# Norm order, fillers and a buffer pool in a four-layer gated cross-attention kernel

## The chip, the cores and the metric

The kernel runs on one core of one Trainium2 chip. The metric is device time in microseconds (us) of one execution; lower is better. The core's engines are TensorE (PE in the profile, with its weight loads as PEld), VectorE (DVE), ScalarE (ACT), GpSimd (POOL) and SyncE (SP, which issues most DMAs).

## What is computed

Two batches of 256 tokens of 256 features (x) pass four layers, each a cross-attention to a context of 2 x 512 rows and a feed-forward, both added to x through a gate. In front of each stands a layer norm.

```python
x = x + tanh(g_xattn[0]) * L0_xattn(layernorm(x), ctx)   # 16 heads, no weights
x = x + tanh(g_ffn[0])   * L0_ffn(layernorm(x), ...)     # ternary weights, SiLU gate
x = x + tanh(g_xattn[1]) * L1_xattn(layernorm(x), ctx, Wq, Wk, Wv, Wo)  # 16 heads of 128
x = x + tanh(g_ffn[1])   * L1_ffn(layernorm(x), ...)     # dense, SiLU gate
x = x + tanh(g_xattn[2]) * L2_xattn(layernorm(x), ctx, ...)  # linear attention
x = x + tanh(g_ffn[2])   * L2_ffn(layernorm(x), ...)     # 8 experts, one for each token
x = x + tanh(g_xattn[3]) * L3_xattn(layernorm(x), ctx, mask)
x = x + tanh(g_ffn[3])   * L3_ffn(layernorm(x), ...)     # shared expert + 2 of 8 experts
```

## The kernel before

The 512 tokens are four tiles of 128 (`n`), two for each batch. All layers are written out one after the other in one function, `flamingo`; each is a chain of products on TensorE into PSUM, evictions and activations on ScalarE, and sums on VectorE. PSUM has two `acc` buffers, four `mm` buffers and two `tr` buffers (for transposes). In SBUF, pools `q4` (11 buffers), `q2` (15) and `q1` (4) are shared by all stages; a tile waits until a buffer of its pool is released.

A scheduler orders the instructions of each engine and places the waits. Where its order is not wanted, the text ties them: `behind(i, j)` puts i after j on the same engine without a wait, and `inline` does so for one instruction after the other. There are three such lines: `line` for VectorE, `pool_line` for GpSimd and `pe_line` for TensorE. An empty list means that the order is free; `append(None)` starts a new line, `clear()` ends it.

The places that the change touches:

- **First feed-forward** (`ternary_ffn`, L660 to L743). Eight chunks `c`. Each has its SiLU, a product with the gate, and `halves` (L370): VectorE cuts the result to its upper bits (`top`), ScalarE copies that as the high half, and GpSimd subtracts for the low half. `l0_down(c)` (L693) multiplies both halves.
- **End of the second attention** (L935 to L1053). The last two heads, 14 and 15, are added to x by tiles: `add14`, `add15` for tiles 0 and 1; `late14`, `late15` for 2 and 3. `norm_stats` (two instructions on VectorE, two on GpSimd for the root) and `norm_apply` (L234) prepare the second feed-forward, `turned1` transposes a tile into `xT`. In between stand constant tables for the routing to come (an iota on GpSimd, L982, its conversion on VectorE, L983, and what is made of it), and the first keys and values of the third attention (`early_products`, `early_keys2`). `pause1` is called inside the feed-forward after its first chunks.
- **Routing** of layer 2 (L1265 to L1340). `busy(cols)` multiplies `ident` by columns of the iota into a part of a PSUM tile that nobody reads. It stands between the norms of tiles 2 and 3, their transposes and their logits. `places` (L1235) then counts rows by experts, `there2` makes a selection matrix, `gather_first` (L1263) gathers rows into `xsT`.
- **Experts of layer 2** (L1421 to L1501). Six quads of four blocks of 32 rows: `l2_up`, `l2_turn`, `l2_down`, `l2_mask`, and `l2_back` (L1471), which multiplies a quad's rows back to the tokens. It sums in two PSUM tiles `y`, tokens' tiles 0 and 1 in one, 2 and 3 in the other.
- **Fourth attention** (L1505 to L1595). `l3_stats(n)` adds y to x and takes the norm's statistics, `norm_apply`, `l3_turned` (L1537), `l3_scores`, `l3_exps` (L1551). The small sum `none` (L1517 to L1521) tells which batch has no valid row. `load_table` runs one activation on a single column so that the table of a function is loaded then.
- **Experts of layer 3** (`l3_down`, L1776). Ten blocks; each is copied from PSUM to a tile `o3` and scattered to DRAM by GpSimd (`scatter`, L1666). All four reads of the scattered rows (L1834) wait for every scatter; the final sums and the stores follow.

Of the kernel before, what the change touches and what calls it, by code (L numbers as in the profile page):

```python
# [25 lines left out]
P = 128  # L26
# [24 lines left out]
def flamingo(ctx: ExitStack, tc: tile.TileContext, a: dict, out: bass.AP):  # L51
# [181 lines left out]
    def norm_apply(n, xn, stats):  # L233
        return inline(nc.vector.tensor_scalar(xn[:, n, :], x[:, n, :], *stats, ALU.subtract, ALU.mult))  # L234
# [37 lines left out]
    def mm(shape=None):  # L272
        return ps_mm.tile(shape or [P, 512], F32, tag="mm", name="mm")
# [95 lines left out]

    def halves(hi, lo, v):  # L370

        top = q2.tile([P, T], F32, tag="q2", name="top")
        i = nc.vector.tensor_scalar(top.bitcast(I32), v.bitcast(I32), -4096, None, ALU.bitwise_and)
        j = nc.scalar.copy(hi, top)
        nc.gpsimd.tensor_sub(lo, v, top)
        return i, j
# [283 lines left out]
    def ternary_ffn():  # L660
# [36 lines left out]
        for c, _, ts in by_batch(FCH):  # L697
# [15 lines left out]
            if ts.stop == T:  # L713
                s = q2.tile([P, T], F32, tag="q2", name="silu")
                silu = nc.scalar.activation(s, ps[c][0], AF.Silu, scale=scales[0])
                nc.vector.tensor_mul(s, s, ps[c][1])
                h = q4.tile([P, 2, T], F32R, tag="q4", name="hT")
                if c > 1:
                    behind(silu, copied, "its product waits for that copy")
                last, copied = halves(h[:, 0, :], h[:, 1, :], s)  # L720
                if c == 1:
                    line.append(last)
                    ternary_signs(1)
                    line.clear()
# [232 lines left out]
    sums = small.tile([P, 2, 1], F32, tag="sum1", name="sum1", bufs=2)  # L957
    nc.scalar.copy(sums, den)
    late14(scale, 2)
    norm_apply(0, xn, stats1[0])  # L960
    late14(scale, 3)
    norm_apply(1, xn, stats1[1])
    scale = l1_scales(sums, 2)
    for n in (2, 3):
        late15(scale, n, 0)
        stats1[n] = norm_stats(n)
    ctx_nat = nat.tile([P, B, 2, 2 * D], F32, tag="nat", name="ctx_nat3")
    ctxT = turned_ctx.tile([P, B, 2, M], F32, tag="ctxT", name="ctxT2")
# [6 lines left out]
    for b in range(B):  # L975
        load_context(nc.sync, ctx_nat, b)


    SL = QUADS * P
    iota = q4.tile([P, SL + 1], F32, tag="q4", name="iota")  # L980
    iota_i = q4.tile([P, SL + 1], I32, tag="q4", name="iota_i")
    nc.gpsimd.iota(iota_i, pattern=[[1, SL + 1]], base=0, channel_multiplier=0)  # L982
    nc.vector.tensor_copy(iota, iota_i)  # L983
    own = small.tile([P, QUADS], F32, tag="own", name="own", bufs=1)
    own_i = small.tile([P, QUADS], I32, tag="own_i", name="own_i", bufs=1)
    nc.gpsimd.iota(own_i, pattern=[[P, QUADS]], base=1, channel_multiplier=1)
    nc.gpsimd.tensor_copy(own, own_i)
    upto = small.tile([P, E, E], F32, tag="upto", name="upto", bufs=1)
    nc.vector.tensor_tensor(upto, iota[:, 0:E].unsqueeze(1).to_broadcast([P, E, E]),
                            iota[:, 0:E].unsqueeze(2).to_broadcast([P, E, E]), ALU.is_le)  # L990

    near1 = small.tile([P, E], F32, tag="near", name="near", bufs=1)
    far = small.tile([P, E], F32, tag="far", name="far", bufs=1)
    nc.vector.tensor_copy(near1, iota[:, 1:512:64])
    nc.vector.tensor_scalar(far, near1, -1.0, 449.0, ALU.mult, ALU.add)
    over = small.tile([P, E], F32, tag="over", name="over", bufs=1)
    nc.vector.tensor_scalar_add(over, near1, 64.0)

    near_r = small.tile([P, NT, E], F32R, tag="near_r", name="near_r", bufs=1)
    nc.vector.tensor_scalar_mul(near_r, near1.unsqueeze(1).to_broadcast([P, NT, E]), 1.0 / P)  # L1000
    fit2 = const.tile([P, 1], F32, name="fit2")
    ids = small.tile([P, 2 * NT], I32, tag="ids", name="ids", bufs=1)
    nc.gpsimd.iota(ids, pattern=[[2 * P, NT], [1, 2]], base=0, channel_multiplier=2)

# [33 lines left out]
    def pause1(ci, b):  # L1038
        if (ci, b) == (1, 0):
            early_keys2(1, *early_products(1))  # L1040
            for n in (2, 3):
                turned1(n)
        if (ci, b) == (1, 1):
            for t in (line, pool_line, pe_line):
                t.clear()

    kv0 = early_products(0)
    for n in (2, 3):
        norm_apply(n, xn, stats1[n])
    for n in range(2):  # L1050
# [251 lines left out]

    busy(384)
    turned = []
    for n in (2, 3):
        norm_apply(n, xn, stats2[n - 2])
        turned.append(logits2(n))
        if n == 2:
            busy(256)
    for fn in turned:  # L1310
        fn()
    busy(384)
    load_dn2(2)
# [107 lines left out]
    def l2_up(q):  # L1421
# [10 lines left out]
        s = q2.tile([P, T], F32, tag="q2", name="silu")  # L1432
        nc.scalar.activation(s, pa, AF.Silu)
        h = q2.tile([P, T], F32, tag="q2", name="h2")
# [8 lines left out]
    def l2_down(q, hT):  # L1443
# [15 lines left out]
        return o  # L1459

    def l2_mask(q):
        back = q2.tile([P, T], F32R, tag="q2", name="back")
        nc.vector.tensor_scalar(back, row, own[:, q : q + 1], None, ALU.is_equal)
        return back

    def l2_back(q, o, back, y):
        for n in range(NT):
            for i in range(2):


                inline(nc.tensor.matmul(y[n // 2][:, n % 2, :], lhsT=back[:, n * P : (n + 1) * P], rhs=o[:, i, :],  # L1471
                                        start=(q == 0 and n % 2 == 0 and i == 0),
                                        stop=(q == QUADS - 1 and n % 2 == 1 and i == 1)), pe_line)

# [4 lines left out]
    for q in range(QUADS + 2):  # L1479
# [18 lines left out]
        if q < QUADS:  # L1498
            hTs[q] = l2_turn(h)
        if q >= 2:  # L1500
            l2_back(q - 2, os.pop(q - 2), backs.pop(q - 2), y)  # L1501
    pe_line.clear()
    late = pair(1, "late").rearrange("p s c -> p (s c)")
# [13 lines left out]
    none = const.tile([P, B], F32, name="none")  # L1517
    p = ps_tr.tile([P, B, 4], F32, tag="tr", name="tr")
    nc.tensor.matmul(p.rearrange("p b c -> p (b c)"), lhsT=ones, rhs=named, start=True, stop=True)
    nc.vector.reduce_sum(none, p, axis=AX.X)  # L1520
    nc.vector.tensor_scalar(none, none, 0.0, None, ALU.is_le)  # L1521

    for t in (line, pe_line):
        t.append(None)
    xn = q4.tile([P, NT, D], F32, tag="q4", name="xn")
# [58 lines left out]
    norm_apply(2, xn, stats3[2])  # L1584
    norm_apply(3, xn, stats3[3])
    l3_turned(0)
    l3_scores(0, ps3[0], slice(0, P), [0])
# [188 lines left out]
    def l3_down(q, hT):  # L1776
        acc = ps_acc.tile([P, D], F32, tag="acc", name="acc")
        for c in range(2):
            for j in range(4):
# [734 lines left out]
```

## Time and profile before

| | us |
|---|---|
| median of 3 runs | 574.4 |
| lowest, highest | 572.72, 577.37 |
| profiled execution | 578.8 |
| its span | 577.1 |
| TensorE busy in the span | 552.9 |
| VectorE, ScalarE, GpSimd busy | 323.9, 227.1, 131.5 |
| mean granted TensorE clock | 0.984 |

The profile is one execution; its span runs from the first instruction to the last. A row of the timeline has the start (us from the span's start), the time in us, engine, line, operation, what it writes and reads with shapes, how many instructions are merged, and in brackets the engine's idle time before it with what ended it. A matrix product in fp32 of 256 columns appears as two instructions. "PEclk" is the granted TensorE clock, in tenths of the full speed on the page and as a fraction in tables by stretches.

### The profile page before, as it was taken

The numbers are of one execution on the slowest core, as the hardware profiler recorded it, in microseconds if no ns is written. First come the engines' busy times: TensorE is split into PE (matmuls) and PEld (weight loads), VectorE is DVE, ScalarE is ACT, GpSimd is POOL, SyncE is SP. The second block draws the span as 40 slices with busy tenths as digits, with TensorE's granted clock in tenths as the row PEclk, the third lists the DMA queues.
The fourth block names the chain that finished last, engine by engine and source line by source line (L and its number), as shares of the span: only waits on it lengthen the run. The fifth ranks groups of instructions, "written<-read, shape, count | busy, mean of one in ns | idle before, by whom it ended". The sixth has DMA issues, their size and how long they took to land.

```text
span 577.1 us, 8662 instructions
## 1 busy us (share of the span) xinstructions
PE 552.9 (96%) x3302; PEld 399.9 (69%) x3302; DVE 323.9 (56%) x744; ACT 227.1 (39%) x465; POOL 131.5 (23%) x227
## 2 busy tenths in 40 slices
PE   8999999999999999999999999999989998999994
PEld 6555665888878788888878776476676456884453
DVE  6968798645475554845555665234566336462323
ACT  6876445643444445344444424113322211522310
POOL 3885444111031101211011123011130002151240
PEclk9999999999999999999999999999997998899998
DMA  7900300000004000130033229630031999313013
GB/s 303 408 5 0 125 22 1 1 1 0 1 0 146 0 2 1 19 128 1 0 147 147 73 72 351 252 147 0 6 141 61 378 420 379 91 45 114 18 44 124
DMA packets 16073, 60.20 MB, mean 104 GB/s; under 512 B 2686, under 2 KB 5957, under 8 KB 12391
## 3 DMA queue, kind: packets, MB, share of 16 engines
q1 hardware_dynamic: 13974, 54.75, 25.3%
q0 software_dynamic: 1472, 4.28, 2.0%
q10 hardware_dynamic: 576, 0.53, 0.3%
q8 instruction: 28, 0.46, 0.3%
q14 instruction: 23, 0.18, 0.1%
HBM read 54.75 MB, written 5.25 MB: 104 GB/s over the span
## 4 chain that ended last, share of the span: by engine, by line
PE 84%; DVE 7%; ACT 2%; issue 2%; POOL 2%; DMA 2%; POOLq 0%; ACTq 0%; DVEq 0%; SPq 0%
PE mm L277 26%; PE acc L277 18%; PE mm L607 8%; PE mm L609 4%; PE mm L1426 4%; PE s L452 3%; PE acc L464 2%; PE q L607 2%; PE mm L1760 2%; PE acc L1447 2%; DVE x L280 2%; PE q L609 1%; PE mm L1263 1%; PE y L1471 1%; PE acc L1782 1%
## 5 line engine op out<-in xcount | busy, mean ns | idle before, releaser
L277 PE MATMUL mm<-qT,kT 128*128 128x256 f32 x256 | 60.7, 380 | 0.0
L277 PE MATMUL acc<-e,v 128*128 128x256 f32 x256 | 60.5, 379 | 0.0
L600 POOL TENSOR_TENSOR h_parts<-w,h_top 128x256 fp32r<-128x256 f32 x28 | 21.8, 779 | 161.6 <-PE acc L277 86.7
L277 PEld LDWEIGHTS mm<-qT,kT 128*128 128x128 f32 x256 | 48.1, 190 | 9.2 <-ACT oT L792 1.6
L277 PEld LDWEIGHTS acc<-e,v 128*128 128x128 f32 x256 | 48.3, 189 | 7.9 <-ACT e L781 0.2
L781 ACT ACTIVATE e<-mm 128x512 f32<-128x512 f32 x64 | 38.0, 597 | 25.8 <-PE mm L277 25.7
L784 DVE TENSOR_TENSOR t<-e,e 128x512 f32<-128x512 f32 x32 | 22.1, 691 | 28.4 <-ACT e L781 28.4
L456 ACT ACTIVATE e<-s 128x512 f32<-128x512 f32 x64 | 32.8, 607 | 6.7 <-PE s L452 5.5
L229 POOL TENSOR_TENSOR rstd<-mv,eps_ln 128x1 f32<-128x1 f32 x30 | 8.1, 270 | 98.6 <-DVE mv L228 98.6
L277 PE MATMUL mm<-xT,ffn 128*128 128x512 f32 (+1 forms) x80 | 28.0, 510 | 1.3 <-ACT xT L1036 1.3
L277 PE MATMUL acc<-w,oT 128*128 128x256 f32 x112 | 27.2, 386 | 2.1 <-ACT oT L792 2.1
L612 ACT ACTIVATE v<-mm 128x512 f32<-128x512 f32 x24 | 14.3, 597 | 33.7 <-PE mm L609 33.7
L613 DVE SCALAR_TENSOR_TENSOR v<-mm,v 128x512 f32<-128x512 f32 x24 | 16.6, 692 | 19.0 <-ACT v L612 19.0
L607 PE MATMUL mm<-ctx_top,h_parts 128*128 128x512 f32 x56 | 27.3, 487 | 0.0
L280 DVE SCALAR_TENSOR_TENSOR x<-acc,gsum,x 128x256 f32<-128x256 f32 x56 | 24.1, 479 | 4.8 <-PE acc L277 4.8
L792 ACT COPY oT<-acc 128x256 f32<-128x256 f32 x32 | 11.9, 372 | 33.4 <-PE acc L277 33.4
L277 PEld LDWEIGHTS acc<-w,oT 128*128 128x128 f32 x112 | 20.7, 190 | 6.3 <-ACT oT L792 3.7
L612 ACT ACTIVATE kT<-mm 128x512 f32<-128x512 f32 x28 | 16.7, 598 | 20.6 <-PE mm L609 20.6
L277 PEld LDWEIGHTS mm<-xT,ffn 128*128 128x128 f32 x80 | 15.0, 190 | 13.6 <-issue 11.0
L452 PE MATMUL s<-w_q,ctx_nat 32*128 32x256 f32 x256 | 21.8, 403 | 2.0 <-ACT e L456 1.1
L613 DVE SCALAR_TENSOR_TENSOR kT<-mm,kT 128x512 f32<-128x512 f32 x28 | 19.3, 689 | 7.2 <-ACT kT L612 7.2
L1426 PE MATMUL mm<-gu,xsT 128*32 128x512 f32 x192 | 22.4, 595 | 0.2 <-ACT xsT L1381 0.2
(393 smaller groups left out, 1162.5 us busy)
## 6 DMA issues: line engine op xcount, KB each, us to landing
gu<-in_l_gu_all SPq DMA_DIRECT2D x16, 1024.0 KB, 7.0
w<-in_l_all SPq DMA_DIRECT2D x4, 2048.0 KB, 13.0
dn<-in_l_dn_all SPq DMA_DIRECT2D x4, 1024.0 KB, 6.2
dn<-in_l_dn_all SPq DMA_DIRECT2D x8, 512.0 KB, 9.7
gu<-in_l_gu SPq DMA_DIRECT2D x4, 704.0 KB, 11.1
ctx_nat<-in_ctx SPq DMA_DIRECT2D x4, 512.0 KB, 13.2
ctxT<-in_ctxT SPq DMA_DIRECT2D x4, 512.0 KB, 5.4
sh<-in_l_sh SPq DMA_DIRECT2D x2, 704.0 KB, 8.5
```

The lines of the kernel that those rows point to most:

```text
L277: inline(nc.tensor.matmul(dst, lhsT=lhsT, rhs=rhs, start=(i == 0), stop=(i == len(pairs) - 1)), pe_line)
L280: return inline(nc.vector.scalar_tensor_tensor(x[:, n, cols], acc, scalar, x[:, n, cols], ALU.mult, ALU.add))
L452: in_turn(nc.tensor.matmul(ps[j][:, k, :], lhsT=ctx_nat[rows, b, hf, c * P : (c + 1) * P], rhs=qm[rows, n, i, :], start=True, stop=True))
L456: exps.append(nc.scalar.activation(es[j], ps[j], AF.Exp))
L600: nc.gpsimd.tensor_sub(dst[1], src, t)
L607: inline(nc.tensor.matmul(same, lhsT=left(i, k), rhs=right(i, k), start=(k == 0 and i == 0), stop=(k == 1 and i == 1)), pe_line)
L609: inline(nc.tensor.matmul(cross, lhsT=left(2, k), rhs=right(2, k), start=(k == 0), stop=(k == 1)), pe_line)
L612: nc.scalar.mul(dst, cross, -EPS * scale)
L613: return inline(nc.vector.scalar_tensor_tensor(dst, same, (1.0 + EPS) * scale, dst, ALU.mult, ALU.add))
L781: nc.scalar.activation(e, s, AF.Exp)
L784: nc.vector.tensor_add(t, es[0], es[1])
L1426: inline(nc.tensor.matmul(ps[j * BLK : (j + 1) * BLK, :], lhsT=xsT[k][:, (4 * q + j) * BLK : (4 * q + j + 1) * BLK], rhs=gu2[home(q, j)][: ...
```

## The change

- `halves` gets the engine of its subtraction as an argument; chunk 0 of the first feed-forward uses VectorE, the others GpSimd as before.
- At the end of the second attention `norm_apply(0)` stands ahead of `late14(2)`, and `norm_apply(1)` ahead of `late14(3)`. The block with `k2`, `v2`, `early_products(0)` and the norms of tiles 2 and 3 moves in the text ahead of the tables; the iota is put behind the last root on GpSimd, its conversion behind the last norm on VectorE.
- In `pause1` the transposes of tiles 2 and 3 stand ahead of the second pair of key and value products.
- In the routing, `busy(384)` becomes twice `busy(256)`; `busy(256)` between the norms becomes `busy(384)`; and `busy(256)` follows each of the two logits, instead of one `busy(384)` after both.
- The last rows of layer 2's experts go back by tiles: quad 4 for tiles 0 and 1, then quad 5 for 0 and 1, then both for 2 and 3. The table of exponentials is loaded after the last SiLU. Three products `ones` x `woT2`, which nobody reads, follow the last of them on TensorE. The sum `none` moves behind the four norms and into the lines.
- `o3` comes from `q2` instead of `q1`.

```diff
-    def halves(hi, lo, v):
+    def halves(hi, lo, v, engine):
...
-        nc.gpsimd.tensor_sub(lo, v, top)
+        engine.tensor_sub(lo, v, top)
...
-                last, copied = halves(h[:, 0, :], h[:, 1, :], s)
+                last, copied = halves(h[:, 0, :], h[:, 1, :], s, nc.gpsimd if c else nc.vector)
...
     nc.scalar.copy(sums, den)
+    norm_apply(0, xn, stats1[0])
     late14(scale, 2)
-    norm_apply(0, xn, stats1[0])
+    norm_apply(1, xn, stats1[1])
     late14(scale, 3)
-    norm_apply(1, xn, stats1[1])
...
+    roots1 = pool_line[-1]
...
     def pause1(ci, b):
         if (ci, b) == (1, 0):
-            early_keys2(1, *early_products(1))
             for n in (2, 3):
                 turned1(n)
+            early_keys2(1, *early_products(1))
...
+    kv0 = early_products(0)
+    for n in (2, 3):
+        normed[:] = [norm_apply(n, xn, stats1[n])]
...
-    nc.gpsimd.iota(iota_i, pattern=[[1, SL + 1]], base=0, channel_multiplier=0)
-    nc.vector.tensor_copy(iota, iota_i)
+    behind(nc.gpsimd.iota(iota_i, pattern=[[1, SL + 1]], base=0, channel_multiplier=0), roots1, "not among the norms")
+    behind(nc.vector.tensor_copy(iota, iota_i), normed[0], "not among the norms")
...
-    busy(384)
+    for _ in range(2):
+        busy(256)
     turned = []
     for n in (2, 3):
         norm_apply(n, xn, stats2[n - 2])
         turned.append(logits2(n))
         if n == 2:
-            busy(256)
+            busy(384)
     for fn in turned:
         fn()
-    busy(384)
+        busy(256)
...
-        nc.scalar.activation(s, pa, AF.Silu)
+        silus[:] = [nc.scalar.activation(s, pa, AF.Silu)]
...
-    def l2_back(q, o, back, y):
-        for n in range(NT):
+    def l2_back(q, o, back, y, tiles=range(NT)):
+        for n in tiles:
...
-        if q >= 2:
+        if 2 <= q < QUADS:
             l2_back(q - 2, os.pop(q - 2), backs.pop(q - 2), y)
+        if q == QUADS:
+            l2_back(4, os[4], backs[4], y, (0, 1))
+            load_table(AF.Exp, silus[0], "the table of exponentials")
+    for tiles in ((0, 1), (2, 3)):
+        if tiles[0]:
+            l2_back(4, os[4], backs[4], y, tiles)
+        l2_back(5, os[5], backs[5], y, tiles)
...
-    for t in (line, pe_line):
-        t.append(None)
+    line.append(None)
+    pe_line.append(last_back[0])
+    warm = mm([P, D])
+    for _ in range(3):
+        chain(warm, [(ones, woT2[:, 0, :])])
...
     norm_apply(3, xn, stats3[3])
+    p = ps_tr.tile([P, B, 4], F32, tag="tr", name="tr")
+    chain(p.rearrange("p b c -> p (b c)"), [(ones, named)])
+    inline(nc.vector.reduce_sum(none, p, axis=AX.X))
+    inline(nc.vector.tensor_scalar(none, none, 0.0, None, ALU.is_le))
...
-        o = q1.tile([P, D], F32, tag="q1", name="o3")
+        o = q2.tile([P, D], F32, tag="q2", name="o3")
```

More of the change, by code (lines that the diff above doesn't have):

```diff
@@ L976, in flamingo @@
         load_context(nc.sync, ctx_nat, b)
[L979 to L982, printed above, removed]
-    nc.vector.tensor_copy(iota, iota_i)
[L984 to L1003, printed above, removed]
     k2 = [q4.tile([P, 4, D], F32, tag="q4", name="k2")]
@@ L1048, in flamingo @@
     for n in (2, 3):
-        norm_apply(n, xn, stats1[n])
+        normed[:] = [norm_apply(n, xn, stats1[n])]
+    SL = QUADS * P
+    iota = q4.tile([P, SL + 1], F32, tag="q4", name="iota")
+    iota_i = q4.tile([P, SL + 1], I32, tag="q4", name="iota_i")
+    behind(nc.gpsimd.iota(iota_i, pattern=[[1, SL + 1]], base=0, channel_multiplier=0), roots1, "not among the norms")
+    behind(nc.vector.tensor_copy(iota, iota_i), normed[0], "not among the norms")
+    own = small.tile([P, QUADS], F32, tag="own", name="own", bufs=1)
+    own_i = small.tile([P, QUADS], I32, tag="own_i", name="own_i", bufs=1)
+    nc.gpsimd.iota(own_i, pattern=[[P, QUADS]], base=1, channel_multiplier=1)
+    nc.gpsimd.tensor_copy(own, own_i)
+    upto = small.tile([P, E, E], F32, tag="upto", name="upto", bufs=1)
+    nc.vector.tensor_tensor(upto, iota[:, 0:E].unsqueeze(1).to_broadcast([P, E, E]),
+                            iota[:, 0:E].unsqueeze(2).to_broadcast([P, E, E]), ALU.is_le)
+    near1 = small.tile([P, E], F32, tag="near", name="near", bufs=1)
+    far = small.tile([P, E], F32, tag="far", name="far", bufs=1)
+    nc.vector.tensor_copy(near1, iota[:, 1:512:64])
+    nc.vector.tensor_scalar(far, near1, -1.0, 449.0, ALU.mult, ALU.add)
+    over = small.tile([P, E], F32, tag="over", name="over", bufs=1)
+    nc.vector.tensor_scalar_add(over, near1, 64.0)
+    near_r = small.tile([P, NT, E], F32R, tag="near_r", name="near_r", bufs=1)
+    nc.vector.tensor_scalar_mul(near_r, near1.unsqueeze(1).to_broadcast([P, NT, E]), 1.0 / P)
+    fit2 = const.tile([P, 1], F32, name="fit2")
+    ids = small.tile([P, 2 * NT], I32, tag="ids", name="ids", bufs=1)
+    nc.gpsimd.iota(ids, pattern=[[2 * P, NT], [1, 2]], base=0, channel_multiplier=2)
     for n in range(2):
@@ L1459, in l2_down @@
         return o
+    last_back = []
     def l2_mask(q):
@@ L1464, in l2_mask @@
         return back
-    def l2_back(q, o, back, y):
-        for n in range(NT):
+    def l2_back(q, o, back, y, tiles=range(NT)):
+        for n in tiles:
             for i in range(2):
-                inline(nc.tensor.matmul(y[n // 2][:, n % 2, :], lhsT=back[:, n * P : (n + 1) * P], rhs=o[:, i, :],
+                last_back[:] = [inline(nc.tensor.matmul(y[n // 2][:, n % 2, :], lhsT=back[:, n * P : (n + 1) * P], rhs=o[:, i, :],
                                         start=(q == 0 and n % 2 == 0 and i == 0),
-                                        stop=(q == QUADS - 1 and n % 2 == 1 and i == 1)), pe_line)
+                                        stop=(q == QUADS - 1 and n % 2 == 1 and i == 1)), pe_line)]
     y = [ps_acc.tile([P, 2, D], F32, tag="acc", name="y2") for _ in range(2)]
@@ L1517, in flamingo @@
     none = const.tile([P, B], F32, name="none")
[L1518 to L1521, printed above, removed]
-    for t in (line, pe_line):
-        t.append(None)
+    line.append(None)
[3 more added lines that the diff above has]
+        chain(warm, [(ones, woT2[:, 0, :])])
     xn = q4.tile([P, NT, D], F32, tag="q4", name="xn")
```

## The prediction

> **What bounds the kernel now.** I read the page first: engine shares, then the clock row.
>
> ```profile
> PE 552.9 (96%) x3302; PEld 399.9 (69%) x3302; DVE 323.9 (56%) x744; ACT 227.1 (39%) x465; POOL 131.5 (23%) x227
> PEclk9999999999999999999999999999997998899998
> ```
>
> TensorE is busy for 96% of the span, and the chain that ended last lies 84% on it. So time can only go where TensorE waits on the chain, where its clock is low, or at the end, where DMA and VectorE carry the chain. The clock row dips near 432 us and near 487 us. To place the dips I asked for TensorE's busy time in stretches of 3.41 us, laid from 431.97 us, where the clock falls (columns: stretch, length, busy with instructions, clock, DMA share, GB/s):
>
> ```profile
> 63.33:66.75 3.42, 2.72 (x11) 1.00 0.00 0
> 350.05:353.46 3.41, 2.74 (x15) 1.00 1.01 416
> 428.56:431.97 3.41, 2.52 (x17) 1.00 0.00 0
> 483.17:486.58 3.41, 1.19 (x11) 1.00 1.02 425
> 486.58:490.00 3.42, 2.93 (x13) 0.51 1.00 268
> ```
>
> Two stretches run at half clock, 432.0 to 438.8 and 486.6 to 493.5, each two stretches long. Each follows a stretch with little TensorE work: 2.52 and 1.19 us of 3.41. Stretches with 2.72 or more are followed by full clock (one with 2.48, in the first attention at 5.31, is too). One product at both clocks, in the timeline:
>
> ```profile
> 427.48 0.39 PE L1263 MATMUL mm<-there,xl 128*128 128x512 f32 x1
> 437.17 0.63 PE L1263 MATMUL mm<-there,xl 128*128 128x512 f32 x1
> ```
>
> Lastly the timeline around each edit, for the waits.
>
> **Part by part, against the profiled execution (578.8 us; span 577.1 and 1.7 around it).**
>
> **First feed-forward.** The low half of chunk 0 goes from GpSimd to VectorE.
>
> ```profile
> 63.81 1.04 DVE L373 TENSOR_SCALAR top<-silu 128x512 int32<-128x512 int32 x1
> 65.00 2.18 POOL L375 TENSOR_TENSOR hT<-silu,top 128x512 fp32r<-128x512 f32 x1 [0.42 <-DVE top L373]
> 67.23 0.97 PE L693 MATMUL outT<-hT,signs 128*128 128x512 f32 x3 [0.95 <-POOL hT L375]
> ```
>
> Chunk 0's low half ends at about 63.9 instead of 64.57 (POOL's 1.30 becomes some 0.69, the row of a 128x512 product on VectorE). But that 0.69 stands before chunk 1's product and cut on VectorE. The cut took 1.04 beside GpSimd's subtraction and 0.43 elsewhere, which gives 0.6 back, so chunk 1 reaches GpSimd near 65.0 as before, and TensorE still waits for GpSimd until 67.2. Ends: 0.5 gained, 0.3 lost; I take 0.
>
> **End of the second attention.**
>
> ```profile
> 345.35 0.79 POOL L982 IOTA iota_i<- 128x769 int32 x1
> 345.49 0.80 DVE L234 TENSOR_SCALAR xn<-x,mv,rstd 128x256 f32<-128x256 f32 x1
> 347.24 3.72 PE L277 MATMUL mm<-xT,ffn 128*128 128x256 f32 x16 [0.46 <-ACT xT L1036]
> 353.64 3.72 PE L277 MATMUL mm<-xT,ffn 128*128 128x256 f32 x16 [0.85 <-ACT xT L1036]
> ```
>
> The second norm took 0.80 beside the iota, 0.41 elsewhere. With the iota behind the last root and the norm ahead of the late sum, it ends near 345.85 instead of 346.29. TensorE is in its kv products until 345.9, and ScalarE has two copies before xT, so only about 0.25 of the 0.45 reaches the 347.24. In the second row, transposes 2 and 3 move ahead of the second pair of kv products (six products, 1.41): these now run while ScalarE copies xT, and the 0.85 goes. The norms they need are ready: without the tables' six VectorE instructions (0.54 for the conversion, some 0.15 to 0.21 each for the rest), the last ends about 350 (before 350.7), and TensorE arrives at 350.7. What is late next is ScalarE's table of SiLU: its exponential ends near 354.4, the load takes 1.28, the first SiLU starts near 355.7, and TensorE needs its buffer at 356.3: no more than 0.1. The moved memset costs POOL 0.24 in idle time; no DMA is moved, and the two zero fills behind the iotas in POOL's queue were issued at 352.9, after an idle of 1.7 that absorbs the iota. Gain 0.25 + 0.85 = **1.1** (ends 0.4 and 1.4).
>
> **Routing.** Ahead of the placing, fillers go from 384+256+384 columns to 256+256, 384, 256, 256: 384 columns more, 0.64 us at the full clock (256 columns take 0.43: eight half products in 1.73). They lie in waits: the first two end at 429.04, and the norm they precede lands at 429.10; the next ends at 430.13, the norm at 430.22; the third fills the 0.43 until xT at 431.45; the last ends near 432.1 and the placing waits for VectorE until 432.75. So they cost nothing at full clock. The stretch before 431.97 had 0.9 idle (0.26, 0.20, 0.43); about 0.4 stays, so busy is near 3.0, over the 2.72 that kept the clock. If it does, the placing (0.8 and 0.8 us of small products) ends 1.0 earlier, the mask at 434.5 instead of 435.5, and eight gathers take 1.72 instead of 3.0: xsT lands near 437.0 instead of 439.9. VectorE's counting, which starts at 436.79, moves 2 us too and its end (440.7) is needed only after 3.57 us of expert products. Gain up to **2.9**; ends 2.9 and a loss of 0.6.
>
> [...]
>
> **Last expert rows and the next attention.**
>
> ```profile
> 486.61 0.63 PE L1537 MATMUL tr<-ident,xn 128*128 128x128 f32 x2 [2.25 <-DVE xn L234]
> ```
>
> Order: the masks of quad 4 for tiles 0 and 1 (four products, 0.48) end at 482.5; quad 5's halves come at 483.04 as before; its four products end about 483.55, against 483.9 now with eight products and the small sum ahead. So x, the norm and the transpose start 0.35 earlier. The other eight products (0.95) and three warm ones (six instructions of 0.216, 1.3) follow to 485.8; the transpose needs its norm at 486.2. The waiting stretch then holds about 2.8 busy instead of 1.19, and the clock should stay up. At full clock: transpose 486.2, xT 487.0, first scores to 487.9, and so on to the third transpose, which waits for the last norm at 490.0; half a group to 491.35; batch 1's sixteen products of 0.216 to 494.8. Now they end at 498.45. So 3.65: **0.35** by order, **3.3** by clock (ends 0 and 3.6 for the latter). Nothing stands behind it: ScalarE has 1.7 us for each two exponentials, and the weights' loads, with 8 to 18 us to landing, end near 494 while the shared experts start at 504. The Exp table (1.28 at 490.63 now) goes into ScalarE's idle time after the last SiLU (475.9 to 479.1). If it is queued just ahead of quad 5's copy (482.63), that copy and the stage come up to 1.3 later. The small sum now holds one of two transpose buffers until VectorE passes the last norm (about 490.2); the second transpose can use the other, freed at 487.0.
>
> **Last rows' pool.**
>
> ```profile
> 560.73 0.37 ACT L199 COPY o<-acc 128x256 f32<-128x256 f32 x1 [4.01 <-remote]
> 561.38 0.97 POOL L1666 DMA_INDIRECT yg<-o,xg_sb  x1 [1.46 <-ACT o L199]
> ```
>
> The tenth copy waits for a buffer that an earlier scatter still reads; TensorE was done at 558.5. With fifteen buffers the copy runs then, and GpSimd's queue limits: scatters follow each 1.28, so the tenth starts at 560.23, not 561.38. All four reads, the additions and the stores wait for it; the shared products end at 568.9, before the last addition would need them (571.1). Gain **1.15** (ends 0.8 and 1.3).
>
> **Sum.** 1.1 + 0.35 + 1.15 = 2.6 in any execution; 2.9 + 3.3 = 6.2 by the clock. From 578.8: 570.0. The profiled execution is 4.4 above the median 574.4 and above the slowest run shown (577.4). If those 4.4 are clock loss that the median run lacks, its loss is 1.8, and 574.4 - 2.6 - 1.8 = 570.0. If they are the profiler's, 574.4 - 8.8 = 565.6. Nothing shown decides; I take the middle, **567.8**, 1.1% under the median.
>
> **Rivals.**
> - All of it counts: 565.6. [...] Chance 0.20.
> - [...] Chance 0.10.
> - Fillers save no clock, or ordinary runs had none to save: 574.4 - 2.6 = 571.8. Against it stand the two dips. Chance 0.07.
> - Slower: the transpose buffer. If the second transpose is given the buffer that the small sum holds, it waits for the last norm, 490.3 instead of 487.9. From 487.0 TensorE has 0.9 of work in 3.3 us, its clock falls there, and the scores' remaining 6.7 us from 490.3 take up to 10.1: 500.4, not 498.45, so this stage loses 2.0 where it should gain. With the 1.1 and the tail's 1.15 kept, and routing as before plus its 0.64 of fillers at half clock (1.3): 574.4 - 2.25 + 2.0 + 1.3 = 575.5. It decides from a 1 us delay of that transpose on. A second half-clock stretch in the PE-bound part after it (3.4 each) would take it past 1%. Against it: buffers are handed out as they come free. Chance 0.11.
>
> The forecast itself has 0.52, with its own range 565 to 570.5. About 1% is what a measurement here tells from no change: 568.7 and 580.1. Faster: 0.43 of the forecast, 0.19 of the first rival, 0.03 of the second, 0.65. Slower: 0.07 of the last. Within: 0.28. The range, 563.5 to 573.0, takes in all but the last rival and the bounds' outer ends.
>
> **What would show it.** Clock at 1.0 through 425 to 505; gathers near 0.4; the scores' end 3.6 earlier against the last back product; no 0.85 before the second feed-forward's second half; the tenth copy right after its product; scatters 1.28 apart to the end; 67.2 unmoved. A dip in either stage, a wait at the second transpose (L1537), or a table load just ahead of the last o2 copy would prove me wrong.

## The result: 571.28 us, and the profile after

| | before | after |
|---|---|---|
| median, us | 573.51 | 571.28 |
| lowest to highest | 572.63 to 577.54 | 570.62 to 572.07 |
| runs | 12 | 12 |
| profiled execution, its span | 578.8, 577.1 | 571.64, 569.9 |
| mean clock in it | 0.984 | 0.999 |

The ratio is 0.9948, with an interval from 0.9928 to 0.9968: faster by half a per cent. It is the ratio of the means, 571.26 and 574.22, which differ by 3.0 us. The changed kernel is 3.5 us above the predicted 567.8 and inside the range of 563.5 to 573.0. The two profiled executions differ by 7.2 us, the medians by 2.2. This difference is the subject of what follows.

The page of the kernel after, engine shares and clock row. No slice of the routing or of the fourth attention is below full clock, where two dips stood before:

```profile
PE 548.9 (96%) x3312; PEld 396.8 (70%) x3312; DVE 323.8 (57%) x745; ACT 229.4 (40%) x468; POOL 129.5 (23%) x226
PEclk9999999999999999999999999999999999999999
```

The stretches of these two places in the kernel after (stretch, length, busy time with instructions of PE, PEld, DVE, ACT and POOL; clock; DMA share; GB/s). Ahead of 432 TensorE is busy for 3.36 us where it was 2.52. The wait ahead of the fourth attention, which begins 3 us earlier here (at 480.2), falls on a stretch with 3.04 busy, where the kernel before had 1.19 from 483.17 on:

```profile
428.54:431.95 3.41, 3.36 (x20) 2.08 (x19) 1.35 (x6) 1.35 (x4) 2.35 (x5) 1.00 0.00 0
479.74:483.15 3.41, 3.04 (x21) 2.82 (x20) 2.40 (x8) 0.38 (x1) 0.76 (x2) 1.00 1.02 425
483.15:486.56 3.41, 2.61 (x22) 2.31 (x21) 2.94 (x10) 0.75 (x2) 2.13 (x6) 1.00 1.08 303
```

The timeline of the kernel after at the places that the prediction worked through:

```profile
68.00 0.95 PE L693 MATMUL outT<-hT,signs 128*128 128x512 f32 x3 [1.10 <-POOL hT L375]
...
353.66 0.70 PE L277 MATMUL mm<-xT,ffn 128*128 128x256 f32 x2 [0.64 <-ACT xT L1010]
...
480.18 1.70 PE L1473 MATMUL y<-o,back 128*128 128x256 f32 x12 [0.37 <-ACT o L1459]
480.96 0.48 DVE L280 SCALAR_TENSOR_TENSOR x<-y,c,x 128x256 f32<-128x256 f32 x1 [0.87 <-PE y L1473]
481.72 1.46 PE L277 MATMUL mm<-woT,ones 128*128 128x256 f32 x6
483.63 0.41 PE L1545 MATMUL tr<-ident,xn 128*128 128x128 f32 x2 [0.34 <-DVE xn L234]
```

Stage by stage in the two profiled executions (starts in us from the span's start):

| landmark | before | after | gained in the stage |
|---|---|---|---|
| first layer's last score, end | 45.81 | 46.46 | -0.65 |
| first feed-forward, last product's end | 86.24 | 86.47 | 0.42 |
| second feed-forward, first product | 347.24 | 347.26 | 0.21 |
| its seventeenth | 353.64 | 353.66 | 0.00 |
| second gather | 436.60 | 434.63 | 1.99 |
| first expert product | 439.95 | 436.96 | 1.02 |
| first back product of quad 4 | 481.98 | 479.07 | -0.08 |
| first transpose of the fourth attention | 486.61 | 483.63 | 0.07 |
| first product of the shared expert | 507.84 | 502.05 | 2.81 |
| its last stage's first product | 558.48 | 552.68 | 0.01 |
| last scatter | 561.38 | 553.93 | 1.65 |

A gain is the difference from the landmark above it. The first row lies ahead of the changed code. A load from DRAM sets its 0.65: VectorE's reduction that waits for the gate's weights (L339) starts at 12.70 before and at 13.35 after. Between the profiles of numbers 4 and 12 below, one and the same program, it moves by 1.1 us. Routing and fourth attention give 5.8 of the 7.2.

### The profile page after: what moved, and what is told of

It reads as the page before. It is cut to its first block, busy times and chain, and to the rows that moved or that the text cites. A ratio compares the mean times of both kernels' runs of the same rounds, so it can differ in the third digit from the quotient of the medians.

```text
span 569.9 us, 8692 instructions
## 1 busy us (share of the span) xinstructions
PE 548.9 (96%) x3312; PEld 396.8 (70%) x3312; DVE 323.8 (57%) x745; ACT 229.4 (40%) x468; POOL 129.5 (23%) x226
## 4 chain that ended last, share of the span: by engine, by line
PE 82%; DVE 8%; DMA 3%; POOL 2%; ACT 2%; issue 2%; SPq 0%; POOLq 0%; ACTq 0%; DVEq 0%
PE mm L277 26%; PE acc L277 19%; PE mm L607 9%; PE mm L609 4%; PE mm L1428 4%; PE q L607 2%; PE mm L1772 2%; PE acc L1449 2%; DMA w<-in_l_gate 2%; DVE x L280 2%; PE acc L464 2%; PE s L452 2%; PE acc L1794 1%; PE q L609 1%; PE mm L1264 1%
```

## The experiments

They are four kernels to a comparison, each comparison on one chip with the kernel before. The kernel before came to 575.95, 574.80 and 575.88 us in the three, against 573.51 above, so each is read against its own. The ratios are those of the record; they go by means and are not the quotients of the medians in their rows.

| kernel | median, us | lowest to highest | lowest clock | runs | ratio to before, interval |
|---|---|---|---|---|---|
| before | 575.95 | 572.57 to 579.06 | 0.984 | 53 | |
| 1 pool alone | 575.7 | 572.19 to 579.02 | 0.984 | 22 | 0.9999 (0.9981 to 1.0017) |
| 2 fillers alone | 573.2 | 572.41 to 575.57 | 0.992 | 17 | 0.9966 (0.9948 to 0.9983) |
| 3 after, no new fillers | 573.67 | 571.51 to 576.33 | 0.989 | 21 | 0.9968 (0.9954 to 0.9983) |
| 4 after, exponential behind | 571.93 | 571.02 to 572.12 | 0.996 | 6 | 0.9925 (0.9906 to 0.9945) |
| before | 574.8 | 571.32 to 578.58 | 0.985 | 32 | |
| 5 after again | 571.47 | 570.97 to 573.59 | 0.994 | 12 | 0.9942 (0.992 to 0.9964) |
| 6 as 4 | 570.68 | 570.03 to 572.22 | 0.993 | 9 | 0.9942 (0.992 to 0.9965) |
| 7 routing's fillers alone | 573.99 | 571.7 to 576.49 | 0.988 | 12 | 0.9999 (0.9978 to 1.0021) |
| 8 unread products alone | 573.58 | 571.1 to 575.19 | 0.992 | 12 | 0.9981 (0.9958 to 1.0003) |
| before | 575.88 | 572.62 to 579.83 | 0.983 | 33 | |
| 9 narrow unread products | 573.9 | 572.42 to 579.28 | 0.986 | 12 | 0.9976 (0.9949 to 1.0003) |
| 10 pool and first feed-forward undone | 573.14 | 572.09 to 575.22 | 0.993 | 12 | 0.9962 (0.9938 to 0.9985) |
| 11 as 4, two more fillers | 572.12 | 570.81 to 572.55 | 0.995 | 10 | 0.9925 (0.9897 to 0.9954) |
| 12 as 4 | 572.39 | 571.26 to 575.89 | 0.991 | 12 | 0.9946 (0.9918 to 0.9973) |

The same program, the kernel before, takes anything from 571.3 to 579.8 us, and the time goes with the mean clock: in the second group 571.32 at 0.999, 574.8 at 0.993, 578.58 at 0.985. Part of the clock's loss costs nothing: all fourteen profiles show half clock again at their end, from 2.5 to 5.3 us after TensorE's last product on (2.8 before, 5.2 after). In the profile of number 12 that alone brings the mean to 0.994. So small differences of the mean clock say little.

### 1. The pool alone

```diff
-        o = q1.tile([P, D], F32, tag="q1", name="o3")
+        o = q2.tile([P, D], F32, tag="q2", name="o3")
```

> The kernel before with the last rows' tile o3 from the pool of 15 buffers, nothing else. Theory A: the tail carries the median's gain, and half-clock stretches are rare in ordinary executions of before. Then the median falls by 1.5 to 1.7 us to about 572.0, the runs still scatter upward to 575 or more, and in the profile the tenth copy follows its product at once and the last scatter starts 1.28 us after the ninth. Theory B: the median's gain comes mainly from the clock, lost in every execution of before, and the tail's gain is hidden by another wait at the end; then the median falls by less than 0.7.

The ratio is 0.9999: no gain is seen, and its interval leaves room for 1.1 us at most. Two more things were seen. The profile of this kernel has no half clock before its end, although it has none of the fillers; the same waits as in the kernel before did not cost the clock here. And the last copy stayed late with the larger pool. The kernel with the pool alone, and below it a kernel with the small pool (number 8), at the last copy and the last scatter:

```profile
550.60 1.93 PE L1782 MATMUL acc<-dn,hT 88*32 88x256 f32 x32 [0.29 <-issue]
553.90 0.37 ACT L199 COPY o<-acc 128x256 f32<-128x256 f32 x1 [3.14 <-PE acc L1782]
554.54 0.98 POOL L1666 DMA_INDIRECT yg<-o,xg_sb  x1 [0.72 <-issue]
```

```profile
550.79 1.93 PE L1787 MATMUL acc<-dn,hT 88*32 88x256 f32 x32 [0.29 <-DVE hT L197]
552.84 0.37 ACT L199 COPY o<-acc 128x256 f32<-128x256 f32 x1 [1.93 <-PE acc L1787]
553.91 0.97 POOL L1671 DMA_INDIRECT yg<-o,xg_sb  x1 [0.30 <-issue]
```

TensorE's products for the copy ended at 552.53 and at 552.72 (start and time of their rows). With the large pool the copy started 1.37 us after that, with the small one 0.12. So a late copy needs no small pool, and a small pool does not by itself make it late.

### 2. The fillers alone, and 3. all but the new fillers

```diff
-    busy(384)
+    for _ in range(2):
+        busy(256)
...
-    for t in (line, pe_line):
-        t.append(None)
+    line.append(None)
+    pe_line.append(last_back[0])
+    warm = mm([P, D])
+    for _ in range(3):
+        chain(warm, [(ones, woT2[:, 0, :])])
```

Number 2 is the kernel before with this, in the old order of the last rows; number 3 is the kernel after with this undone.

> The kernel before with the routing's fillers and the three unread products behind the last back products, in the old order of those; nothing else. Theory A: the median falls by 0.5 at most (573.5 to 573.0), and only the slow tail of the runs goes: highest below 574.5, clock 0.997 or more in every run. Theory B: the median falls by 2 us or more. If the fillers lie on the path, the median rises by 0.3 to 1.

> The changed kernel with the old fillers (384, 256, 384) and without the three unread products; nothing else undone. Theory A: median 571.3 to 571.8 and runs scattering up to 575 with clocks of 0.985 to 0.99. Theory B: median 573 or more.

Their medians are 2.8 and 2.3 us below the kernel before, by the ratios about 1.9 us, and they differ by 0.5 us, which their scatter hides. By the medians that is theory B for both. Number 2 missed its bounds for the long executions: 575.57 and clock 0.992, where 574.5 and 0.997 were set. Each cuts off the long executions, the fillers more so: lowest clock 0.992 and 0.989 against 0.984. What makes the new order help without fillers is not shown. The profile of number 3 still has both dips. Its stretches, around them:

```profile
419.97:423.38 3.41, 2.64 (x18) 2.01 (x16) 2.10 (x12) 0.62 (x1) 0.14 (x1) 1.00 0.95 382
423.38:426.79 3.41, 3.41 (x10) 2.88 (x11) 2.04 (x6) 0.00 (x0) 0.00 (x0) 0.50 0.03 12
481.41:484.82 3.41, 1.69 (x14) 1.39 (x12) 3.00 (x9) 0.04 (x1) 1.56 (x4) 1.00 1.06 427
484.82:488.23 3.41, 3.03 (x14) 3.03 (x15) 2.56 (x10) 0.70 (x2) 1.67 (x5) 0.50 1.03 223
```

Each dip lasts one stretch here, two in the kernel before; number 7 below, in the old order, has them one stretch long too. The first one stands at 423.4, not at 432. In the profile of the kernel before the clock changes at 432.04, 438.86, 486.65, 493.48 and 571.98, which lie 2, 14, 2 and 23 times 3.41 us apart: its two dips start 54.61 us apart, 16 times 3.41, those of numbers 3 and 7 61.44, 18 times. So the stretches of 3.41 us lay differently over the program in these executions. The 2.64 busy ahead of the first dip still lies between the prediction's 2.52 and 2.72; number 7 has one that does not.

### 4. The exponential behind the copies

In the kernel after, the exponential of the first keys (L987) is tied behind ScalarE's copies of the transposed tiles 2 and 3.

```diff
-        nc.scalar.activation(t, t, AF.Exp)
+        i = nc.scalar.activation(t, t, AF.Exp)
+        if copied1:
+            behind(i, copied1.pop(), "not ahead of the copies")
...
-        positives(k2[0][:, mt, :], z, negatives(z))
+        return lambda: positives(k2[0][:, mt, :], z, negatives(z))
...
-                turned1(n)
-            early_keys2(1, *early_products(1))
+                copied1[:] = [turned1(n)]
+            finish0[0]()
+            early_keys2(1, *early_products(1))()
...
```

> The changed kernel with one order altered on ScalarE: the exponential of the first keys (L987) is put behind the copies of the third and fourth tiles' xT, which it now stands in front of. Theory: that exponential, which waits for VectorE behind the constant tables, is the wait that took the place of the 0.85 us at the second half of the second feed-forward. Then this half starts 0.8 us earlier against the first half, and the median falls by 0.8 from the changed kernel's. Rival: ScalarE would be late anyway (its SiLU table, or the second products' buffers), and the median moves by less than 0.2.

The reason is in the timeline of the kernel after. The transposes do stand ahead of the key products now, but on ScalarE the exponential stands in front of the copies. The transposes start at 350.82; the exponential waits until 352.65 for VectorE, which works through the tables first, and the copies run behind it, from 352.98 on:

```profile
350.15 0.79 POOL L1027 IOTA iota_i<- 128x769 int32 x1
350.22 0.86 DVE L234 TENSOR_SCALAR xn<-x,mv,rstd 128x256 f32<-128x256 f32 x1 [0.71 <-POOL rstd L230]
351.33 0.55 DVE L1028 CAST iota<-iota_i 128x769 f32<-128x769 int32 x1
352.34 0.28 DVE L986 TENSOR_SCALAR fm<-z 128x256 f32<-128x256 f32 x1
352.65 0.42 ACT L987 ACTIVATE fm<-fm 128x256 f32<-128x256 f32 x1 [5.45 <-DVE fm L986]
352.98 0.63 ACT L1010 COPY xT<-tr 128x256 f32<-128x256 f32 x2
```

In the experiment's second run (number 6) the copies run as soon as the transposes are done, the exponential starts at the same time as before, and TensorE no longer waits:

```profile
351.23 0.83 ACT L1014 COPY xT<-tr 128x256 f32<-128x256 f32 x2 [4.03 <-PE tr L1013]
352.66 0.42 ACT L989 ACTIVATE fm<-fm 128x256 f32<-128x256 f32 x1 [0.60 <-DVE fm L988]
352.88 1.68 PE L277 MATMUL mm<-xT,ffn 128*128 128x256 f32 x7
```

From the first product of the feed-forward to the seventeenth: 6.40 us in the kernel after, 5.63 here and 5.61 in number 4. The 0.8 us is shown in the stage. The median of number 4, 571.93, is no lower than the 571.28 of the kernel after in another comparison, so the two were run side by side.

### 5 and 6. After, and after with the exponential behind, side by side

> The changed kernel itself, beside the kernel before in the same hours, because the kernel before came out at 575.95 us in the last comparison and at 573.51 in the one that the change was measured in. If the loss at half clock is what differs from one execution to the next, the changed kernel stays between 570.6 and 572.1 us whatever the kernel before does here, and the ratio falls below 0.995 wherever the kernel before loses more: at 575.9 it would be 0.993. If the gain were a fixed number of microseconds (2.2), the changed kernel would follow the kernel before and the ratio would stay at 0.996.

> The changed kernel with the exponential of the first keys tied behind ScalarE's copies of the transposed tiles 2 and 3, now beside the changed kernel. If that exponential is the wait that took the place of the 0.85 us, the run is 0.8 us below the changed kernel, and the seventeenth product of the feed-forward starts 5.6 us after the first instead of 6.4. If the wait is of no account because ScalarE's SiLUs are late next, the time is the same as the changed kernel's to 0.2 us.

The kernel after stayed where it was (571.47 against 571.28), while the kernel before moved by 1.3 us. So the gain is no fixed number of microseconds: 2.2 in one comparison, 3.3 in the other. A line fitted to time against clock puts the kernel before at 571.6 and the kernel after at 570.7 for a clock of 1. This is rough, for the reason given on the mean clock, but it makes most of the 3.3 a matter of the clock. The profiles say the same: number 8 below is the kernel before but for three unread products, and its profile has no dip either. From the end of the first layer's scores to the last scatter it takes 508.15 us, the kernel after 507.47. So about 0.7 is gained at full clock.

With the exponential behind, the median is 0.8 lower and the profile ends 0.9 earlier. Resampling the runs gives the difference of the medians an interval from -1.4 to +0.7, and the ratio to the kernel before is 0.9942 for both: shown in the stage, not in the time of the whole.

### 7 and 8. Each kind of filler alone

Number 7 is the kernel before with the first part of the fillers' diff (the `busy` calls), number 8 with the second (the three unread products).

> The kernel before with the new fillers of the routing alone (256, 256, 384, 256 and 256 columns), all else as it was. If each filler guards its own stage, the first dip goes and the second stays: least time 572.5 us, the most loaded executions 3 us below the kernel before's 579, mean clock no lower than 0.989. If fillers in the routing only move the dip to the next stage, or the loss comes in one stage alone, the spread is that of the kernel before.

> The kernel before with the three products that nobody reads, ahead of the next attention's transposes, alone. If each filler guards its own stage, the second dip goes and the first stays: least time 572.5 us, the most loaded executions 3.3 us below the kernel before's 579. If the products stand behind the small sum and so only fill TensorE's queue after the wait, nothing changes. Together with the routing's fillers alone this says which of the two was worth more.

Neither alone is told from no change: 0.9999 and 0.9981, both intervals with 1 in them. Their longest executions are shorter (576.49 and 575.19 against 578.58), out of 12 against 32. Number 8's profile has no dip. Number 7 was expected to have no dip in the routing. Its profile has one, one stretch long, and one in the fourth attention. The first follows the stretch from 420.80 to 424.21, where no filler is added:

```profile
420.80:424.21 3.41, 2.76 (x18) 2.08 (x16) 2.10 (x12) 0.56 (x1) 0.28 (x1) 1.00 0.96 387
424.21:427.62 3.41, 3.29 (x10) 2.82 (x11) 2.18 (x6) 0.06 (x1) 0.00 (x0) 0.50 0.02 8
...
482.24:485.65 3.41, 1.16 (x9) 0.81 (x8) 3.03 (x10) 0.00 (x0) 1.42 (x4) 1.00 1.02 424
485.65:489.06 3.41, 2.95 (x14) 2.89 (x14) 2.55 (x8) 0.72 (x2) 1.80 (x5) 0.50 1.09 257
```

It went to half clock after a stretch with 2.76 busy, more than the 2.72 that the prediction took for safe; 2.53 in number 8 (428.06 to 431.47) and 2.06, twice in a row, in number 1 (from 479.11 to 485.94) were followed by full clock. So busy time does not tell these stretches apart. What TensorE did from 420.80 on says what may:

```profile
421.45 0.25 PE L1235 MATMUL acc<-near_r,ones 128*128 128x16 f32 x1 [0.35 <-DVE ksum L1124]
421.55 0.26 PE L1235 MATMUL acc<-route,before 128*128 128x16 f32 x1
421.66 0.25 PE L1235 MATMUL acc<-route,ones 128*128 128x8 f32 x1
421.97 1.03 PE L277 MATMUL den<-ks,qry 128*128 128x8 f32 x8
422.86 1.11 PE L277 MATMUL mm<-qry,kv 128*128 128x256 f32 x4
```

Eleven products of 8 or 16 columns count 1.5 us as busy and have 104 columns in all. I added up, for all stretches of the fourteen profiles, only the time of products of more than 32 columns (time in which two products overlap counts for the earlier one). Most of the stretches with little of it:

| kernel, stretch | busy | of that in wide products | clock after it |
|---|---|---|---|
| before, 483.24 to 486.65 | 1.17 | 1.09 | half |
| 3, 419.97 to 423.38 | 2.65 | 1.15 | half |
| 7, 482.24 to 485.65 | 1.17 | 1.17 | half |
| 7, 420.80 to 424.21 | 2.76 | 1.26 | half |
| 1, 421.08 to 424.50 | 2.96 | 1.46 | full |
| 4, 419.60 to 423.01 | 3.00 | 1.50 | full |
| 3, 481.41 to 484.82 | 1.69 | 1.57 | half |
| 8, 421.23 to 424.64 | 3.00 | 1.58 | full |
| 9, 479.83 to 483.25 | 3.06 | 1.60 | half |
| before, 428.62 to 432.04 | 2.53 | 1.64 | half |
| 6, 420.58 to 424.00 | 3.00 | 1.73 | full |
| 1, 482.52 to 485.94 | 2.05 | 2.05 | full |
| 8, 428.06 to 431.47 | 2.53 | 2.14 | full |

No stretch at full clock with more than 1.64 us of wide products was followed by half clock, and none with less than 1.46 by full clock. Between the two it goes either way. The ends of products are modelled: with the overlaps given to the wide products, the values rise by up to 0.15 us.

Among the stretches that already run at half clock the values lie higher. In the kernel before, 2.48 us of wide products (432.04 to 435.45) and 2.95 (486.65 to 490.06) were followed by a second one at half clock, which makes its dips two stretches long; 2.95 in number 7 and 3.02 or more in the other stretches were followed by full clock. Two halves of an unread product of 384 columns, in the kernel before, at full and at half clock:

```profile
428.18 0.81 PE L1301 MATMUL acc<-iota,ident 128*128 128x384 f32 x2
431.97 1.56 PE L1301 MATMUL acc<-iota,ident 128*128 128x384 f32 x2
```

If the times at half clock are halved for that, 1.24 and 1.48 stand against 1.48 or more, which fits the values at full clock. It is an estimate from nine stretches.

### 9. The same busy time in narrow products

```diff
-    for _ in range(3):
-        chain(warm, [(ones, woT2[:, 0, :])])
+    for _ in range(6):
+        chain(warm[:, 0:8], [(ones, woT2[:, 0, 0:8])])
```

> The changed kernel with its three unread products of 256 columns (six instructions, 1.3 us) made into six unread products of 8 columns (twelve instructions of about 0.11 us, 1.3 us): TensorE is as busy, but streams hardly anything. In the traces so far half clock follows a stretch of 3.41 us in which products of more than 32 columns took 1.64 us or less, also where narrow ones fill it to 2.65 or 2.76. If columns count, the dip behind the last expert rows comes back in those executions whose stretch falls on it, some half of them: the times spread upward from 571 to 574 or 575, and the median is 1 to 2 us above the changed kernel's 571.4. If busy time counts, as the prediction's sums had it, nothing moves: median 571.4, mean clock 0.997.

The median, 573.9, is 0.75 above number 10 of the same comparison (interval by resampling 0.2 to 1.3), which itself gives up 0.4 of the kernel after in the first feed-forward. The kernel after was not run beside these two, so the expected 1 to 2 us above it can't be read off; its 571.47 of another comparison is no measure, since numbers 10 and 12 came out later than expected too. Of twelve executions one took 579.28, at clock 0.986. The profile caught the dip. The unread products, then the stretch that holds them and the one after it:

```profile
480.86 1.40 PE L277 MATMUL mm<-woT,ones 128*128 128x8 f32 x12
```

```profile
479.83:483.25 3.42, 3.06 (x26) 2.76 (x25) 2.98 (x9) 0.03 (x1) 1.54 (x4) 1.00 1.02 427
483.25:486.66 3.41, 3.02 (x14) 3.02 (x15) 2.56 (x10) 0.71 (x2) 1.68 (x5) 0.50 1.06 228
```

TensorE was busy for 3.06 of 3.42 us, 90%, with 1.60 in wide products, and half clock followed. With the wide fillers, both profiles of the kernel after stay at full clock here; the first has 3.05 and 2.49 us in wide products (479.74 to 483.15 and 483.15 to 486.56). So six instructions of 256 columns, 1.46 us, kept the clock in these profiles, and twelve of 8 columns, 1.40 us, did not in this one.

### 10. Pool and first feed-forward undone

```diff
-                last, copied = halves(h[:, 0, :], h[:, 1, :], s, nc.gpsimd if c else nc.vector)
+                last, copied = halves(h[:, 0, :], h[:, 1, :], s, nc.gpsimd)
...
-        o = q2.tile([P, D], F32, tag="q2", name="o3")
+        o = q1.tile([P, D], F32, tag="q1", name="o3")
```

> The changed kernel with two parts undone that lie far apart and are read apart in the trace: the last rows' pool of fewer buffers, and chunk 0's low half of the first feed-forward on GpSimd. If the larger pool was worth nothing, as the trace of the kernel with the three unread products alone says (last scatter 1.25 us after the shared experts' first last-stage product, with the small pool), the last scatter starts 1.25 to 2.1 us after that product, as in the changed kernel on the same chip; by the prediction's 1.15 it would be 2.4 or more. If the feed-forward's part is real, its last outT product ends 0.44 us later against the end of the first layer's scores than in the changed kernel (40.45 instead of 40.01 us after it). Median 571.4 plus 0.4 if only the second holds, plus 1.6 if both.

From the end of the first layer's scores to the last product of the first feed-forward: 40.40 us here, 40.43 before, 39.99 to 40.01 in the profiles of the kernel after. So VectorE's subtraction in chunk 0 is worth 0.4. The median, 573.14, is 1.3 above the 571.8 that was expected for this; the last copy is late here, by the next paragraph 0.9 of it, and the rest is not explained.

For the pool, the last scatter's start after the first last-stage product of the shared expert, in all profiles: with the small pool 2.90 (before), 2.13 (2), 1.25 (7), 1.25 (8), 2.13 (10); with the large one 1.25 (after), 2.07 (1), 2.10 (3), 2.10 (4), 1.25 (5), 1.26 (6), 2.08 (9), 2.09 (11), 2.78 (12). All four profiles of the comparison with numbers 5 to 8 have 1.25 or 1.26, with either pool, and all eight of the other two have 2.07 or more, with either pool. So in the experiments the value goes with the comparison and not with the pool. Before and after, 2.90 and 1.25, are the one pair that would fit the pool. Number 12, with the large pool, even shows the wait of the kernel before:

```profile
553.10 0.37 ACT L199 COPY o<-acc 128x256 f32<-128x256 f32 x1 [3.84 <-remote]
553.75 0.97 POOL L1683 DMA_INDIRECT yg<-o,xg_sb  x1 [1.38 <-ACT o L199]
```

What makes the copy late in some executions, by up to 1.65 us in the last scatter, stays open.

### 11 and 12. Two more fillers, at 421 and 424 us

Number 12 is number 4 once more, number 11 adds to it:

```diff
+    def fill_wait(dst):
+        inline(nc.tensor.matmul(dst, lhsT=ident, rhs=iota[:, 0 : dst.shape[-1]], start=True, stop=True), pe_line)
...
+            fill_wait(rs.rearrange("p a b c -> p (a b c)")[:, 0:160])
...
     summary2(1)
+    fill_wait(lgt_all[:, 256:416])
```

> The changed kernel with the exponential of the first keys behind the copies, and two more fillers of 160 columns in the two waits of 0.36 us near 421 and 424 us, where two traces had a stretch that half clock followed (1.15 and 1.26 us of wide products in it). At full clock it costs nothing: least time as without them, 570.0 to 570.6. If these waits are the last place where the clock falls, no execution is below clock 0.996 and the highest is below 571.8; if the narrow products around them are too many for two fillers, the highest stays at 572 or more.

> The kernel that the one with two more fillers is compared with: the changed kernel with the exponential of the first keys behind the copies. 570.7 us median as in its last comparison, with a few executions at 572 and more where a stretch falls on 420 to 424 us.

The fillers are free: the second gather is 0.03 us later against a start that is 0.05 later. The highest time falls from 575.89 to 572.55 and the lowest clock rises from 0.991 to 0.995; the mean is 0.9 lower (interval by resampling 0.1 to 1.8), the medians differ by 0.3 (not told apart). The bounds that were set were missed: the highest is 572.55, not below 571.8, and by the expectation 572 or more would say that two fillers are too few; but number 12 itself came out 1.7 higher than expected, so this can't be decided. The clock's bound of 0.996 could not tell: the profile has 0.996 without a dip, from its end alone. At 0.9925 of the kernel before (interval 0.9897 to 0.9954), number 11 beats that kernel; the kernel after had 0.9948 and 0.9942, and was not run beside it, so that it beats this one too is likely from the stage of 0.8 and the cut of the long executions, but not shown.

Number 12 missed its expected 570.7 by 1.7. At equal clock, 0.997, its five executions took 571.26 to 572.43, those of number 6 took 570.30 and 570.57. Neither profile has a dip, and number 12's has the last scatter 1.5 us later than number 6's against the shared expert's products, by the row above; that this is the reason is argued from one profile of each, not shown.

## Why the prediction was right or wrong

**Direction and range held, the size did not.** The gain is 2.2 us of a forecast 6.6, and 571.28 lies outside the forecast's own range of 565 to 570.5. The wide range, 563.5 to 573.0, held because it had been drawn to take in most rivals, not because the sum was right. By the 1% bound that was set, the outcome is "within 1%", which had 0.28. The nearest rival in number is "fillers save no clock, or ordinary runs had none to save", 571.8, with a chance of 0.07. Its number is near by luck. It keeps 2.6 of gain in any execution and none by the clock; the runs show about 0.7 of the first, and the clock made up most of the rest.

**Two steps failed: from the profiled execution to the median, and the fixed terms.** The 6.6 were 2.6 in any execution and 4.0 by the clock; the 2.2 are about 0.7 and 1.5. The first step: the clock's 6.2 was well worked out for the profiled execution: 3.0 in the routing (2.9 said) and 2.8 in the fourth attention (3.3 said). But 578.8 was near the top of what the kernel before does (579.83 in 130 executions), since it had both dips at double length, 6.83 us. Of the two readings, "those 4.4 are clock loss that the median run lacks" was the right one; taking the middle added 2.2. With that reading the clock was worth 1.8, close to the 1.5. One profile could not tell how often the dips come, and the middle let a half of that doubt count as gain. Nor does all of the 6.2 count in every execution, as the first rival has it: in number 1 the wait ahead of the fourth attention fell on two stretches, each kept 2.06 us of work, and the clock stayed at 1.00.

**The fixed 2.6 were 0.7.** Its terms, each against the profiles:

- First feed-forward: 0 taken, 0.4 measured, inside the ends of 0.5 and -0.3. The wait at 67.2 stayed, as said (68.00, or 67.35 with the later start taken off); that TensorE gives other products to the wait (four from 65.58 on, before two from 65.42) and has less left afterwards (six from 68.79, before eight from 68.04) was missed.
- End of the second attention: 0.25 said and 0.21 measured for the first half; 0.85 said and 0 measured for the second. What was late next was not ScalarE's table but its exponential, in the queue ahead of the copies. The prediction followed the transposes on TensorE and the norms on VectorE, and didn't ask what stood ahead of the copies on the third engine of that chain. Number 4 got the 0.8 back in the stage.
- Last expert rows: 0.35 said by order, 0.07 measured. The first four products after the halves' wait were put at 0.48; the sum that waits for them starts 0.78 after the first product, as it did before (0.76, 483.17 to 483.93). And the eight products that left the path had been in TensorE's waiting time anyway.
- Pool: 1.15 said, nothing measured (number 1). One row with "remote" as releaser was taken for the buffer; the same row is there with the larger pool. The 1.65 in the table of stages is the late copy, whose cause stays open.

**What held.** The new fillers cost nothing that shows at full clock (from the first gather to the first expert product 12.4 us in the kernel after, 424.52 to 436.96, and 12.4 in number 8 with the old ones); the first expert product comes 3.0 earlier; the table of exponentials is loaded at 473.00, right after the last SiLU; the second transpose of the fourth attention is not held up by the small sum, so the slower rival did not come about. "Clock at 1.0 through 425 to 505" held for both profiles of the kernel after, but probably not for every execution: two of the twelve of number 5 took 573.5 and 573.6, at a mean of 0.994.

**Waits and busy time.** Half clock followed a stretch whose longest wait was 0.43 us (before, from 428.6 on) and one in which TensorE was busy for 90% (number 9, from 479.83 on). To go by the rows was right; to read them as busy time was not. Where the dips fall differed between the profiles: the kernel before has them at 432.0 and 486.7, number 7, its near copy, at 424.2 and 485.7, number 1 has none before its end.

## What to carry to other kernels

When a kernel's time scatters with the clock, a single profiled execution is one draw: place it within the spread of times first, and count a dip only by how often it comes. Where TensorE's clock falls behind a wait, try wide products in the wait, not narrow ones (here 1.46 us of 256 columns kept the clock, 1.40 us of 8 columns did not), and judge the filling by the time in wide products in any stretch as long as the shortest dip, 3.41 us here: at full clock, more than 1.64 of it was followed by full clock in all fourteen profiles. After moving work on one engine, walk the queue of each engine behind it, above all for an instruction that stands ahead in order and waits for a third one.

## What the runs showed of the hardware

- Half clock came in dips of 3.41 or 6.83 us. In the kernel before the changes of the clock lie 2, 14, 2 and 23 times 3.41 us apart; the two dips of an execution start 16 (before) or 18 (3, 7) times 3.41 apart. Where they fall differed between the profiles (first dip at 432.0, 424.2 and 423.4). Two-stretch dips cost 2.8 to 3.0 us here, one-stretch dips about 1.2 to 1.3 (number 7 against number 8: 13.6 and 12.4 us from the first gather to the first expert product, 24.3 and 23.1 from quad 4 to the shared expert).
- At full clock, in the fourteen profiles of these kernels, stretches of 3.41 us with less than 1.46 us of products of more than 32 columns were followed by half clock, those with more than 1.64 by full clock; in between both were seen. Products of 8 columns took 0.11 us each, and twelve of them did not keep the clock (number 9, one profile).
- The last copy of a chain that needs nothing but TensorE's products started 1.4 to 2.2 us after they ended in nine of fourteen profiles and 0.1 us after in the five others. In the experiments this went by comparison and not by kernel; its cause is open.
